# A decoder layer on one core: where the minimum over two key halves and the first experts' pieces stand in the engines' order

## The chip, the core and the metric

The kernel runs on one core of one Trainium2 chip. The metric is the device time of one execution in microseconds (us), the median of three runs. The core has five engines with instruction queues of their own, each worked off in order: TensorE (PE in the profile; its weight loads are shown apart as PEld), VectorE (DVE), ScalarE (ACT), GpSimd (POOL) and SyncE (SP), which here mostly issues DMA transfers. They meet only at semaphores.

## The reference, cut to what matters

One layer with three parts works on x of shape (4, 1024, 256): a gated recurrent scan, a cross attention on a short context, and a transformer block with causal attention and a mixture of experts. The change touches the end of the causal attention and the start of the experts:

```
scores = jnp.einsum('bhqd,bhkd->bhqk', q, k) / hd ** 0.5        # 16 heads of 16
scores = jnp.where(causal, scores, -jnp.inf)
attn = jax.nn.softmax(scores, axis=-1)
o = jnp.einsum('bhqk,bhkd->bhqd', attn, v)...
a = o @ Wo + bo + x
h2 = _ln(a, ln2_g, ln2_b)
logits = h2 @ Wr + br                                            # 8 experts
topv = jax.lax.top_k(logits, TOP_K)[0]                           # 2 of them
w = jax.nn.softmax(jnp.where(logits >= topv[..., -1:], logits, -jnp.inf), axis=-1)
mid = jax.nn.gelu(jnp.einsum('bsd,edf->bsef', h2, e_w1) + e_b1, approximate=False)
moe = jnp.einsum('bse,bsed->bsd', w, jnp.einsum('bsef,efd->bsed', mid, e_w2) + e_b2)
return moe + a
```

## The kernel before, in words

**Stages.** The scan works in eight blocks of 512 tokens (to about 600 us in the profile), the cross attention follows (to about 1050 us), then the causal attention (to about 1877 us), then the experts. All engines but SP run in an order that the program writes out by hand; from the experts' start SP's too.

**Attention units.** A unit is one block of 512 queries (BLK) with a group of four heads (c, four groups); there are 32 units of cross attention and 32 causal ones. Of the eight causal units of a sequence, four belong to its first half of the queries (512 keys) and four to the second (1024 keys). Each unit has two lists of jobs. The *search* (largest) finds for each query the greatest score: matmuls into a score tile of PSUM (ps_max, L825), for the diagonal keys the mask added by DVE (L830), then a reduce on DVE with the sign turned (L832). For the second half of the queries it takes the keys in two parts: results for the first 512 go to m (mpad), those beyond to a tile twice, and the minimum of both (a maximum, as the signs are turned) is L836. Then put() (L834 to L841) transposes m on PE with an identity (shift, L839) and DVE adds the result to the queries (qs, L841). The *weighing* makes the scores again with these shifted queries (ps_exp, L896), takes the exponential on ACT (L898), cuts the diagonal on POOL (L902) and multiplies with the values (ps_o, L866). The search and the score products share three score tiles of PSUM (tag sc).

**Order of jobs.** The main loop runs the weighing of unit u step by step and, beside it, the search of unit u+1, which is ahead by LEAD = 5 jobs (find). put() of a unit is issued as soon as two search jobs of the following unit have been issued:

```
if min(begins[put[0] + 1] + 2, len(search)) <= found[0]:
    units[put[0]][0][1]()
```

The sixteen searches of a unit with 1024 keys are sorted by width and turned by five, so a unit ends and the next one begins with widths of 384, 256 and 128 keys. Around these lists, other jobs (norms, projections, output products, routing) are filled in from the lists ahead, urgent, behind and norms.

**After the last unit.** Twelve jobs with matmuls of the last block remain in urgent and behind: four back (L918), two transposes of on (L758), two output products two (L946, whose sum v DVE adds in L949), two transposes of the normalised rows (L758), choose with the router product (L1280), and places with the ranks (L1308, L1309). Between the eighth and the ninth stand nine jobs without matmuls, the norm of v: four statistics (L1010, L1011), the root (DVE L132, then a power on POOL, L133), its product (L1026), two scalings on ACT (L1032), and an end mark. rows (a DMA on SP, L1260, and copies on POOL) stands ahead of choose; two totals (POOL, L1267) and gates (DVE, L1297 to L1303) stand between choose and places; two totals, place and eight scatters on POOL (sent, L1337) stand behind.

**The first experts' pieces.** Four blocks of 256 rows (firsts_), whose rows are known before the last block is routed, are worked off in pieces between these jobs. A part is two of eight hidden columns (hidden, L1604, with Gelu on ACT, L1607) or four of eight products of the second layer (second, L1614); it counts. A with_ entry counts nothing and follows at once: added (two DVE operations, L1623 and L1624, and a scatter on POOL, L1627), load (five DMA loads on SP, L1551 to L1569), addressed (L1582, L1584) and turned (transposes on PE, L1592, and DVE, L1593). The list holds hidden of blocks 0 and 1 (eight parts), results of 0 and 1 (eight parts, 9 to 16; with added after parts 10, 12, 14 and 16, and load and turn of block 2 after 12, of block 3 after 16), then hidden and results of 2 and 3 (sixteen parts). some(n) issues n counting parts; what is left is issued after the tables of the remaining blocks (L1701 to L1770), and then the main loop over those blocks begins (L1775 on).

## Time and profile before

| | |
|---|---|
| median of three runs | 2412.08 us (2404.89 to 2424.54) |
| profiled execution, its own time | 2414.23 us |
| its span, first to last instruction | 2412.5 us |
| TensorE, mean granted clock | 0.955 |
| busy: TensorE, VectorE, ScalarE, GpSimd | 95%, 55%, 42%, 18% |

All times below are those of the profiled execution, counted from the start of its span. A row of the order of time has start, duration, engine, line, operation, what it writes and reads, and how often it was repeated without a break; in brackets stands how long the engine sat idle before it and what ended that. The granted clock is the share of TensorE's full clock that it was given.

### The profile page before, as it was taken

Reading aid. Unit: us, or ns where it says so; the run is one execution under the profiler, and the core shown is the slowest. Engines: PE = TensorE matmul, PEld = TensorE weight load, DVE = VectorE, ACT = ScalarE, POOL = GpSimd, SP = SyncE. Lnnn points to the kernel's source line nnn. Section 1 sums busy time; section 2 is a strip of 40 time slices with the busy share of each in tenths; the row PEclk is TensorE's granted clock in tenths of the full one; section 3 lists DMA queues with packets and bytes.
Section 4 is the critical chain, followed back from the end, with each engine's and each line's share of the span. In section 5 each row is a group of like instructions: output and inputs, shape, how many; then the busy total and the mean of one; then the engine's idle time right before and its main releaser. Section 6 shows DMA issues by size and latency. Waiting matters only on the chain. (4 is left out here: it accounts for less than half of the span.)

```text
span 2412.5 us, 35625 instructions
## 1 busy us (share of the span) xinstructions
PE 2280.5 (95%) x13356; PEld 1358.8 (56%) x13356; DVE 1315.2 (55%) x2742; ACT 1014.1 (42%) x1541; POOL 440.3 (18%) x642
## 2 busy tenths in 40 slices
PE   6999999998899999999999999999899899999998
PEld 2666666666545555343344334333433678888887
DVE  5767666667545554467667767765866231111111
ACT  3453344443345555354554455354435322222222
POOL 3100000000201011021132224133223222222222
PEclk9999999999889999899999899899989999999999
DMA  8970000000100010000111010001001556766666
GB/s 213 280 194 1 1 1 1 1 1 1 41 19 13 20 27 16 19 23 10 32 32 36 19 36 19 28 27 52 10 27 35 174 156 198 203 193 186 192 203 201
DMA packets 136288, 177.30 MB, mean 73 GB/s; under 512 B 33156, under 2 KB 109292, under 8 KB 136108
## 3 DMA queue, kind: packets, MB, share of 16 engines
q1 hardware_dynamic: 113900, 122.80, 16.5%
q0 software_dynamic: 21696, 51.79, 9.0%
q8 instruction: 109, 1.79, 0.3%
q14 instruction: 71, 0.58, 0.1%
q10 hardware_dynamic: 512, 0.34, 0.1%
HBM read 101.98 MB, written 60.33 MB: 67 GB/s over the span
## 5 line engine op out<-in xcount | busy, mean ns | idle before, releaser
L898 ACT ACTIVATE pt<-ps_exp 128x1024 f32<-128x1024 f32 (+4 forms) x512 | 438.1, 861 | 479.0 <-PE ps_max L825 260.8
L896 PE MATMUL ps_exp<-qs,kT 32*128 32x512 f32 (+4 forms) x2048 | 501.5, 586 | 5.8 <-DVE mpad L832 1.8
L825 PE MATMUL ps_max<-kT,qa 32*128 32x512 f32 (+3 forms) x1536 | 359.1, 559 | 7.5 <-ACT pt L898 3.5
L832 DVE TENSOR_REDUCE mpad<-ps_max 128x2 f32<-128x1024 f32 (+3 forms) x256 | 261.0, 1025 | 96.3 <-PE ps_max L825 91.2
L1607 ACT ACTIVATE mid<-ps,bias 128x256 f32<-128x256 f32 (+1 forms) x296 | 133.0, 459 | 357.9 <-PE ps L1604 335.7
L896 PEld LDWEIGHTS ps_exp<-qs,kT 32*128 32x128 f32 (+1 forms) x2048 | 147.7, 181 | 238.0 <-issue 136.5
L1604 PE MATMUL ps<-hT,w 128*128 128x256 f32 (+1 forms) x1184 | 250.1, 369 | 4.2 <-DVE hT L1593 3.7
L1614 PE MATMUL ps<-w,mid 128*128 128x256 f32 x1104 | 251.4, 381 | 2.1 <-DMA w<-in_L_ffn_e_w_dram 2.1
L866 PE MATMUL ps_o<-pt,vs 128*32 128x512 f32 (+4 forms) x2048 | 246.7, 549 | 2.0 <-POOL pt L902 1.6
L1604 PEld LDWEIGHTS ps<-hT,w 128*128 128x128 f32 x1184 | 214.0, 192 | 33.7 <-DVE hT L1593 4.2
L1614 PEld LDWEIGHTS ps<-w,mid 128*128 128x128 f32 x1104 | 207.4, 191 | 29.2 <-DMA w<-in_L_ffn_e_w_dram 2.7
L902 POOL TENSOR_SCALAR_AFFINE_SELECT pt<-pt 128x256 f32<-128x256 f32 x256 | 104.1, 408 | 526.0 <-ACT pt L898 524.9
L1627 POOL DMA_INDIRECT out_dram<-y,to x69 | 107.1, 1552 | 404.4 <-DVE y L1624 370.7
L814 DVE TENSOR_REDUCE mpad<-ps_max 128x4 f32<-128x616 f32 x128 | 102.2, 800 | 143.7 <-PE ps_exp L896 101.4
L830 DVE TENSOR_TENSOR ps_max<-ps_max,mask_qk 128x256 f32<-128x256 f32 x256 | 109.6, 428 | 89.7 <-PE ps_max L825 81.4
L825 PEld LDWEIGHTS ps_max<-kT,qa 32*128 32x128 f32 x1536 | 124.4, 194 | 58.6 <-ACT pt L898 28.1
L1582 DVE CAST to<-xr 128x2 int32<-128x2 f32 (+1 forms) x37 | 6.1, 166 | 247.1 <-DMA xr<-routed 245.7
L323 PE MATMUL ps_xz<-xnT,w_in 128*128 128x512 f32 x256 | 124.0, 611 | 0.5 <-ACT xnT L315 0.3
L866 PEld LDWEIGHTS ps_o<-pt,vs 128*32 128x32 f32 (+1 forms) x2048 | 42.1, 110 | 132.7 <-issue 103.3
L340 PE MATMUL ps_a<-w,w_a 128*128 128x512 f32 x256 | 115.9, 593 | 0.0
L810 PE MATMUL ps_max<-kT,qa 32*128 32x154 f32 x1024 | 107.0, 331 | 3.4 <-ACT pt L898 1.8
L832 DVE TENSOR_REDUCE twice<-ps_max 128x2 f32<-128x768 f32 (+3 forms) x128 | 105.5, 824 | 4.4
(328 smaller groups left out, 3026.2 us busy)
## 6 DMA issues: line engine op xcount, KB each, us to landing
w<-in_L_ffn_e_w_dram SPq DMA_DIRECT2D x74, 1024.0 KB, 7.2
routed<-zero POOLq DMA_DIRECT2D x16, 2080.0 KB, 53.0
xr<-routed SPq DMA_DIRECT2D x32, 260.0 KB, 6.8
qa<-close SPq DMA_DIRECT2D x248, 32.0 KB, 1.9
last<-in_L_ffn_e_b_dram SPq DMA_DIRECT2D x37, 128.0 KB, 4.0
kT<-close SPq DMA_DIRECT2D x128, 32.0 KB, 2.0
plain<-row SPq DMA_DIRECT2D x8, 512.0 KB, 4.9
out_dram<-xs SPq DMA_DIRECT2D x8, 512.0 KB, 2.9
```

The costliest lines, as they stand in the source:

```text
L323: nc.tensor.matmul(ps, w_in[:, k, c * P : (c + 1) * P], xnT[:, k, :], start=k == 0, stop=k == 1)
L340: nc.tensor.matmul(ps, w_a[:, k, c * P : (c + 1) * P], w[:, k, :], start=k == 0, stop=k == 3)
L825: nc.tensor.matmul(ps[:, i, : s1 - s0], qT[r, j * P : (j + 1) * P], kT[r, c, s0:s1], start=True, stop=True)
L830: nc.vector.tensor_add(x, x, mask_qk.unsqueeze(1).to_broadcast([P, 2, P]))
L832: nc.vector.tensor_reduce(to, ps[:, :, : s1 - s0], AX.X, ALU.max, negate=True)
L866: nc.tensor.matmul(o[0][g * HP : (g + 1) * HP, off:], vs[:n, kt, (4 * c + g) * HV : (4 * c + g) * HV + HP], pts[g // 2][:n, g % 2, off:], ...
L896: nc.tensor.matmul(ps[:n, i, off:], kT[r, c, k0 : k0 + n], shifted[0][r, off:], start=True, stop=True)
L898: nc.scalar.activation(pt[:n, :, off:], ps[:n, :, off:], AF.Exp, scale=HD**-0.5)
L1604: nc.tensor.matmul(ps[:, :mb], self.w1[:, k, f * P : (f + 1) * P], self.hT[:, k, :mb], start=k == 0, stop=k == 1)
L1607: nc.scalar.activation(self.mid[:, f, :mb], ps[:, :mb], AF.Gelu, bias=self.bias[:, f : f + 1])
L1614: nc.tensor.matmul(self.ps, self.mid[:, f, j * P : (j + 1) * P], self.w2[:, f, :], start=f == 0, stop=f == FF // P - 1)
L1627: nc.gpsimd.indirect_dma_start(out=rows, out_offset=bass.IndirectOffsetOnAxis(ap=self.to[:, j_], axis=0), in_=y, in_offset=None, bounds_ch ...
```

## The change

The minimum L836 is taken out of put(). In units with a second key part, the last search job of the unit is wrapped: it runs and then issues the minimum. So on DVE's queue the minimum stands directly behind its unit's last reduce; the transposes and the add of put() stay where they were.

In the loop over the last block's jobs, some() stands ahead of each job with matmuls and no longer behind it, and the list of counts has one entry more: 18 parts are issued in the loop, 17 before.

```
--- before.py
+++ after.py
@@ -831,9 +831,12 @@
                 to = twice[:, j, 2 * pair : 2 * pair + 2] if s0 else m[:, j, 2 * pair : 2 * pair + 2, HD]
                 nc.vector.tensor_reduce(to, ps[:, :, : s1 - s0], AX.X, ALU.max, negate=True)
 
+            def last(job):
+
+                job()
+                nc.vector.tensor_tensor(m[:, :, :, HD], m[:, :, :, HD], twice, ALU.min)
+
             def put():
-                if twice is not None:
-                    nc.vector.tensor_tensor(m[:, :, :, HD], m[:, :, :, HD], twice, ALU.min)
                 tp = mm_tile("shift")
                 for j in range(NJ):
                     nc.tensor.transpose(tp[:, j * P : (j + 1) * P], m[:, j].rearrange("p g i -> p (g i)"), ident)
@@ -852,6 +855,8 @@
                 for i in range(len(parts)):
                     _, j, s0, pair = parts[(i - LEAD) % len(parts)]
                     jobs.append(lambda j=j, s0=s0, pair=pair: many(j, s0, pair))
+            if twice is not None:
+                jobs.append(lambda job=jobs.pop(): last(job))
             return jobs, put
 
         waiting, urgent, ahead, behind = [], [], [], []
@@ -1684,12 +1689,11 @@
                 if not _:
                     n -= 1
 
-        some(1)
-        gaps = [1, 1, 1, 2, 1, 1, 1, 3, 1, 1, 3]
+        gaps = [1, 1, 1, 1, 2, 1, 1, 1, 4, 1, 1, 3]
         for job in urgent + behind:
+            if job.mm:
+                some(gaps.pop(0))
             job.do()
-            if job.mm and gaps:
-                some(gaps.pop(0))
 
         rp = ss.enter_context(tc.tile_pool(name="r_tab", bufs=1))
```

More of the change, by code (lines that the diff above doesn't have):

```diff
@@ L832, in many, with last @@
                 nc.vector.tensor_reduce(to, ps[:, :, : s1 - s0], AX.X, ALU.max, negate=True)
+            def last(job):
+                job()
+                nc.vector.tensor_tensor(m[:, :, :, HD], m[:, :, :, HD], twice, ALU.min)
             def put():
-                if twice is not None:
-                    nc.vector.tensor_tensor(m[:, :, :, HD], m[:, :, :, HD], twice, ALU.min)
                 tp = mm_tile("shift")
@@ L854, in largest @@
                     jobs.append(lambda j=j, s0=s0, pair=pair: many(j, s0, pair))
+            if twice is not None:
+                jobs.append(lambda job=jobs.pop(): last(job))
             return jobs, put
@@ L1685, in some @@
                     n -= 1
-        some(1)
-        gaps = [1, 1, 1, 2, 1, 1, 1, 3, 1, 1, 3]
+        gaps = [1, 1, 1, 1, 2, 1, 1, 1, 4, 1, 1, 3]
         for job in urgent + behind:
+            if job.mm:
+                some(gaps.pop(0))
             job.do()
-            if job.mm and gaps:
-                some(gaps.pop(0))
         rp = ss.enter_context(tc.tile_pool(name="r_tab", bufs=1))
```

## The prediction, made before the changed kernel was run

> **What bounds the kernel now.** I read the page first, then the windows by stage, then the waits and the order of time around the lines that the diff touches. The page says that TensorE (PE) is the bound almost everywhere.

> ```profile
> span 2412.5 us, 35625 instructions
> PE 2280.5 (95%) x13356; PEld 1358.8 (56%) x13356; DVE 1315.2 (55%) x2742; ACT 1014.1 (42%) x1541; POOL 440.3 (18%) x642
> ```

> The min (L836) stands in the causal attention, 1050 to 1862 us. Windows there, one after the min of 1142.4 us, one after that of 1747.2 us, and the expert start (columns: stretch, length, busy time and instructions of PE, PEld, DVE, ACT, POOL, granted clock, DMA share, GB/s):

> ```profile
> 1050.00:1862.00 812.00, 762.65 (x5183) 321.63 (x5183) 568.44 (x1146) 382.04 (x537) 212.32 (x401) 0.94 0.09 27
> 1142.00:1158.00 16.00, 15.38 (x108) 6.36 (x108) 10.89 (x22) 6.68 (x10) 1.51 (x4) 1.00 0.08 17
> 1749.00:1767.00 18.00, 17.49 (x84) 8.25 (x84) 9.92 (x25) 5.03 (x7) 3.14 (x5) 0.53 0.09 30
> 1877.00:1964.00 87.00, 72.12 (x351) 61.07 (x349) 32.70 (x143) 24.44 (x45) 23.40 (x29) 0.92 0.53 155
> ```

> PE is idle for 49 of 812 us, and its clock is sometimes halved: 0.53 over 18 us. The waits (engine, line, releaser; total, times, longest), and one of them in order of time:

> ```profile
> PE shift L839 <- DVE mpad L836: 26.2, 16, 2.3
> PE shift L839 <- ACT close L774: 2.4, 1, 2.4
> ```
> ```profile
> 1786.03 0.42 DVE L830 TENSOR_TENSOR ps_max<-ps_max,mask_qk 128x256 f32<-128x256 f32 x1
> 1786.49 0.69 DVE L832 TENSOR_REDUCE twice<-ps_max 128x2 f32<-128x512 f32 x1
> 1787.10 0.17 DVE L836 TENSOR_TENSOR mpad<-mpad,twice 128x16 f32<-128x16 f32 x1
> 1787.33 0.66 PE L839 MATMUL shift<-ident,mpad 128*128 128x128 f32 x4 [1.57 <-DVE mpad L836]
> 1788.02 0.69 DVE L841 TENSOR_TENSOR qs<-qa,shift 128x512 f32<-128x512 f32 x1 [0.75 <-PE shift L839]
> ```

> The min is ready to run once its unit's last reduce is done (here 1784.8), but it stands behind two search jobs of the next unit. PE has run those two searches and stands at the shift transposes for 1.57 us. Over half of the stage's idle time is these 16 waits. At the expert start PE stands still twice, and the norm starts late:

> ```profile
> 1901.30 0.69 DVE L949 TENSOR_TENSOR v<-v,wo 128x512 f32<-128x512 f32 x1 [2.77 <-PE wo L946]
> 1908.26 0.42 DVE L1010 BATCH_NORM_STATS2 bnst<-v 128x6 f32<-128x256 f32 x1
> 1912.69 1.95 PE L758 MATMUL tp<-ident,row 128*128 128x128 f32 x4 [5.81 <-ACT row L1032]
> 1933.35 0.19 PE L1706 MATMUL n_extra<-extra,ones 128*128 128x1 bf16 x1 [6.10 <-DVE extra L1703]
> 1964.30 0.80 PE L1604 MATMUL ps<-hT,w 128*128 128x256 f32 x1 [2.58 <-DVE hT L1593]
> ```

> **Part 1, the min.** Nothing is added or removed: 16 mins of 0.17 us, each moved ahead of two mask adds (0.42) and reduces (0.69 to 0.96). What it is moved past on DVE is delayed by 0.17 us; PE waits for those reduces only for a free score tile, of which there are three. PE's order is unchanged, and no DMA, ScalarE, SP or POOL instruction moves. (a) The wait. PE reached the transposes 1.2 to 2.0 us before the min, and the last reduce had ended 2.3 to 4.4 us before it, so the whole 26.2 us can go. Next late is DVE: behind the put it runs the shift add (0.69), then mask add and reduce of three short searches (1.1, 0.85, 0.85), 3.5 us, while PE needs about 3.0 for them and already loses 0.2 to 0.6 there. The shift add comes only some 0.9 us earlier, so PE will give part of its 1.6 us back. Bounds 12 and 26; I take 20. The score products that need the shift come over 3 us later, so its add stays covered.

> (b) The clock. The trace's record of the granted clock knows two values, 1 and 0.5. Ten of the sixteen puts are followed, within 6 us of the min, by a stretch at half clock: 10.2, 17.1, 6.8, 6.8, 17.1, 3.4, 6.8, 3.4, 17.1, 10.2 = 98.9 us. Puts without a min are the control: 43 of 48 show no gap at their transposes, four have 0.25 to 0.75 us and no half clock behind them, and one waits 2.4 us for ACT (L774) and has half clock behind it. So in this stage the stretches hang on the waits. One sign is against that: of four router groups (L1280) at full clock three are followed by none, but the one at 1429.2 us stands right ahead of the stretch of 1431.7 us. Their price: 16 router matmuls take 1.95 us at full and 3.58 at half clock, so at most 0.46 of a stretch is lost, 45 us. From first to second put of a batch it is 38.0 us with 10.2 us of half clock and 41.1, 40.9, 39.9 with 17.1: 2.6 us for 6.9, 0.38 each. From second to third, 36.6 with none, 35.9 with 6.8, 36.9 with 3.4: nothing seen. So 71.7 us of long stretches at 0.38 is 27, 27.2 us of short ones at 0.15 (between none and 0.46) is 4: 31 us if all go. Bounds 0 and 45; as the short waits that may be left (0.25 to 0.75) brought none, I take 28.

> [...]

> **Part 2, the pieces.** The last block's jobs hold twelve with matmuls; pieces stood behind each, now in front. Between neighbours that is the same place: ahead of the first eight 1, 2, 3, 4, 6, 7, 8 and 9 pieces are done in both kernels. Ahead of the ninth (row transposes) it is 12 before and 13 after, of the tenth 13 and 14, of the router 14 and 15, of the ranks 17 and 18. What differs in order: pieces 10 to 12 (second-layer products with two added(), the load and the turn of block 2), and one more, stand behind the nine norm jobs and not ahead of them; one piece stands before the router, and three behind the gates. (c) Norm: v is complete at 1901.99, but DVE reaches the statistics at 1908.26, behind two added() (0.42+0.35 each) and the turn (0.16+0.16+0.99), which wait for PE. Now it starts at 1902.0, and the rows end 5.86 us later (as 1908.26 to 1914.12), at 1907.9. PE meanwhile runs four pieces of 1.78 us (24 matmuls took 5.34) and the turn's 0.6, to 1908.8: no wait, 0.9 us to spare. Before, the transposes ended at 1914.64 with three pieces done; now at 1909.4 with four: 5.2+1.8. PE also ran 6.8 us from 1909.6 at half clock (piece 13: 2.88 us against 1.89), another 0.7. Sum 7.7. (d) Ranks no longer wait 0.54 for the turn on DVE, and kept, whole, reciprocal and gate (1927.08 to 1928.25) run ahead of the ranks: 1.1 off the 6.10. Sum 9.3. (e) Given back: the main blocks need the table too. It moves by place, 9.3 less the one piece more that now lies ahead of the ranks, 1.8: 7.5, through eight scatters on POOL (1.27 each) and DVE's table work. The first main rows would be late by up to 1.8, half of it within the 2.58 of PE idle that is there anyway: I take 8.5, bounds 4 (the norm not covered) and 10. On SP the order is the same (load 2, plain rows, load 3, output rows), on POOL the norm's power is ahead of two scatters, and two totals ahead of one; POOL is idle before them. On ACT no Gelu lies in pieces 9 to 16.

> **Sum.** 20 + 28 + 8.5 = 56.5 off the profiled 2414.2 (span 2412.5 and 1.7 around it) is 2357.7; that execution is 2.1 above the median of three, so 2356.

> **The rivals.** A: the half clock stays, brought about by the short, thin matmuls at each unit's end and not by the wait. For it: the router at 1429.2 us, and in the scan a gap of only 0.39 us (PE L381 at 205.05 us, among matmuls with 16 rows of weights) is followed by half clock; against: the 43 puts. Then 20+8.5: 2412-28.5 = 2384. [...] B: the wait is replaced: PE stops one or two matmul groups later, at the score tile that the same two reduces free. For it: DVE is busy 70% of the stage and waits of PE on it are there (0.2 to 0.6). Against: three tiles, of which two are free by then. The puts give 5, the clock nothing: 2412-13.5 = 2398. C, slower: as B, but the wait now lies whole in one of the clock's windows at all 16 puts and not at 10: six more stretches of 17.1 at 0.38 are 39, less the tail's 8.5: 2442. It decides from two more long stretches (13 against 8.5). That the change does not do what it says is left out: the min is issued with its job.

> **How the numbers follow.** Forecast 0.70, with a range of its own of 2335 (26+41+10 off the 2412) to 2378 (20+10+4 off); A 0.15, B 0.10, C 0.05. The range of 8 in 10 reaches to A: 2335 to 2390. One per cent, about what a measurement of this kernel can tell from none (its three runs lie 0.8% apart), is 2388 and 2436. Faster: the forecast and most of A, 0.82; within: the rest of A and B, 0.13; slower: C, 0.05.

> **What would show it.** Right: no wait of the shift transposes on DVE (26.2 before); a granted clock above 0.98 in the attention stage (0.94); transposes of the rows without the 5.81 wait, and 5 us left of the 6.10. Wrong: half-clock stretches behind puts without a wait (A), or a new wait of scores or searches for DVE of 15 to 25 us (B, C).

## The result, and the profile after

The changed kernel takes 2381.89 us (median of four runs, 2381.47 to 2384.16), the kernel before 2412.65 us beside it (2404.89 to 2424.54): a ratio of 0.987, interval 0.983 to 0.991. That is 30.8 us less, inside the range of 2335 to 2390, but 26 us above the forecast of 2356. Run again later, the same kernel took 2381.91 us, and there the ratio was 0.984 (0.980 to 0.989), as the kernel before took 2424.28 on that chip.

The profiled execution after took 2381.52 us. Its page begins:

```profile
span 2379.8 us, 35650 instructions
PE 2266.9 (95%) x13356; PEld 1353.4 (57%) x13356; DVE 1313.7 (55%) x2742; ACT 1013.7 (43%) x1541; POOL 441.1 (19%) x642
```

I compare by stages that begin and end at the same instruction in both kernels. "Causal" runs from the first shift transposes of a causal unit to the first transposes of expert rows. Its windows, before and then after (stretch, length, busy time of PE, PEld, DVE, ACT, POOL, granted clock, DMA share, GB/s):

```profile
1017.10:1877.57 860.47, 809.85 (x5500) 339.44 (x5498) 594.44 (x1206) 413.54 (x581) 228.35 (x429) 0.93 0.10 29
```

```profile
1021.04:1850.56 829.52, 794.46 (x5500) 333.00 (x5499) 592.50 (x1206) 414.48 (x583) 228.55 (x429) 0.96 0.10 30
```

The same 5500 matmuls take 31.0 us less. PE's idle time in them is the length less the busy time: 50.6 us before, 35.1 after, so 15.5 us are waits. The other 15.5 us are busy time, and the change that the trace shows there is the clock: it is at half speed for 114.3 us of this stage before and for 63.0 after (from the trace's record of the granted clock). All stages (PE idle is counted between PE's first and last instruction):

| stage | before: us, PE idle, half clock | after: us, PE idle, half clock | difference |
|---|---|---|---|
| scan | 637.5, 25.3, 45.4 | 640.4, 25.2, 51.3 | +2.9 |
| cross | 379.6, 14.7, 34.9 | 380.6, 14.9, 35.9 | +1.0 |
| causal | 860.5, 50.6, 114.3 | 829.5, 35.1, 63.0 | -31.0 |
| tail, to n_extra | 55.8, 12.6, 10.1 | 52.9, 8.4, 7.0 | -2.9 |
| rest of the experts | 479.1, 5.8, 11.5 | 476.4, 6.4, 5.4 | -2.7 |

These are one profile of each kernel, and the split depends on which execution was taken. The profile of changed_again (the changed kernel once more, below) has 838.6 us for the causal stage, with 37.6 us of PE idle time and 69.9 us of half clock: 21.9 us less than before, 13.0 of them waits. The experiments below widen this. The nine profiles without added matmuls differ in this stage by the place of the min (the late last put of three of them aside). The two with the min late take 860.5 and 869.4 us, the seven with it early 829.5 to 851.0. On the mean the stage is 27.8 us shorter, 17.3 of them PE idle time.

The waits of PE after (engine, line, releaser; total, times, longest); line numbers are up to five higher than before, and the transposes of put() are now L842:

```profile
PE ps_exp L901 <- DVE twice L832: 6.0, 12, 0.9
...
PE n_extra L1710 <- DVE extra L1707: 5.7, 1, 5.7
PE tp L1597 <- DMA xr<-routed: 4.8, 3, 2.1
PE ps_max L825 <- DVE twice L832: 3.5, 5, 1.2
...
PE shift L842 <- DVE mpad L837: 2.1, 1, 2.1
```

Of the sixteen waits of the shift transposes one is left. In its place stand short waits of the score products and searches for the reduces (twice, L832): 9.5 us, against 2.3 before in the two lines below.

```profile
PE ps_exp L896 <- DVE twice L832: 1.5, 3, 0.9
PE ps_max L825 <- DVE twice L832: 0.8, 1, 0.8
```

In order of time, a put of the kernel after (compare the one at 1787.33 before):

```profile
1760.60 0.96 DVE L832 TENSOR_REDUCE twice<-ps_max 128x2 f32<-128x768 f32 x1
...
1761.59 0.18 DVE L837 TENSOR_TENSOR mpad<-mpad,twice 128x16 f32<-128x16 f32 x1
...
1761.69 0.42 DVE L830 TENSOR_TENSOR ps_max<-ps_max,mask_qk 128x256 f32<-128x256 f32 x1
1761.70 0.48 PE L901 MATMUL ps_exp<-qs,kT 32*128 32x256 f32 x2 [0.39 <-DVE twice L832]
...
1762.46 0.66 PE L842 MATMUL shift<-ident,mpad 128*128 128x128 f32 x4
...
1764.08 0.68 DVE L844 TENSOR_TENSOR qs<-qa,shift 128x512 f32<-128x512 f32 x1
...
1765.98 0.38 PE L901 MATMUL ps_exp<-qs,kT 32*128 32x128 f32 x2 [0.79 <-DVE twice L832]
...
1768.64 0.63 PE L871 MATMUL ps_o<-pt,vs 128*32 128x256 f32 x4 [1.60 <-POOL pt L907]
```

The min stands directly behind its unit's last reduce, and the transposes wait for nothing. But 3.5 us later PE waits 0.79 us for a score tile that a later reduce has to free, and at 1768.64 it waits 1.60 us for the cut of an exponential: PE is now ahead of the other engines by what it no longer loses at the transposes, and gives part of that back a little later.

The start of the experts after:

```profile
1875.93 0.69 DVE L954 TENSOR_TENSOR v<-v,wo 128x512 f32<-128x512 f32 x1 [2.77 <-PE wo L951]
1876.54 0.42 DVE L1015 BATCH_NORM_STATS2 bnst<-v 128x6 f32<-128x256 f32 x1
...
1883.08 0.60 PE L758 MATMUL tp<-ident,row 128*128 128x128 f32 x4
...
1885.38 0.38 SPq L1556 DMA_DIRECT2D xr<-routed  x1
...
1893.18 0.63 PE L1597 MATMUL tp<-ident,xr 128*128 128x128 f32 x4 [2.09 <-DMA xr<-routed]
...
1903.41 0.19 PE L1710 MATMUL n_extra<-extra,ones 128*128 128x1 bf16 x1 [5.68 <-DVE extra L1707]
```

The statistics stand right behind v, where 6.3 us lay before, and the transposes of the rows no longer wait 5.81 us. New is the wait of 2.09 us at 1893.18: the turn of block 3 comes earlier on PE, and its rows, whose load is issued at 1885.38, have not landed. The wait ahead of n_extra is 5.68 us, against 6.10.

### The profile page after: what moved, and what is told of

Same layout as the page of the kernel before. It is cut to its first block, busy times and chain, and to the rows that moved or that the text cites. A ratio compares the mean times of both kernels' runs of the same rounds, so it can differ in the third digit from the quotient of the medians.

```text
span 2379.8 us, 35650 instructions
## 1 busy us (share of the span) xinstructions
PE 2266.9 (95%) x13356; PEld 1353.4 (57%) x13356; DVE 1313.7 (55%) x2742; ACT 1013.7 (43%) x1541; POOL 441.1 (19%) x642
## 5 line engine op out<-in xcount | busy, mean ns | idle before, releaser
L901 PE MATMUL ps_exp<-qs,kT 32*128 32x512 f32 (+4 forms) x2048 | 490.6, 572 | 10.2 <-DVE twice L832 6.0
L825 PE MATMUL ps_max<-kT,qa 32*128 32x512 f32 (+3 forms) x1536 | 351.0, 546 | 8.9 <-DVE twice L832 3.5
L832 DVE TENSOR_REDUCE mpad<-ps_max 128x2 f32<-128x1024 f32 (+3 forms) x256 | 261.1, 1025 | 92.6 <-PE ps_max L825 87.3
L871 PE MATMUL ps_o<-pt,vs 128*32 128x512 f32 (+4 forms) x2048 | 240.6, 535 | 3.1 <-POOL pt L907 2.7
L830 DVE TENSOR_TENSOR ps_max<-ps_max,mask_qk 128x256 f32<-128x256 f32 x256 | 109.5, 428 | 83.4 <-PE ps_max L825 76.6
L832 DVE TENSOR_REDUCE twice<-ps_max 128x2 f32<-128x768 f32 (+3 forms) x128 | 105.5, 825 | 4.4
```

Source lines behind the costliest of these rows:

```text
L825: nc.tensor.matmul(ps[:, i, : s1 - s0], qT[r, j * P : (j + 1) * P], kT[r, c, s0:s1], start=True, stop=True)
L830: nc.vector.tensor_add(x, x, mask_qk.unsqueeze(1).to_broadcast([P, 2, P]))
L832: nc.vector.tensor_reduce(to, ps[:, :, : s1 - s0], AX.X, ALU.max, negate=True)
L871: nc.tensor.matmul(o[0][g * HP : (g + 1) * HP, off:], vs[:n, kt, (4 * c + g) * HV : (4 * c + g) * HV + HP], pts[g // 2][:n, g % 2, off:], ...
L901: nc.tensor.matmul(ps[:n, i, off:], kT[r, c, k0 : k0 + n], shifted[0][r, off:], start=True, stop=True)
```

## The experiments

Theory at the start: the gain is the waits (some 16 us net), the clock (some 15 us: short waits of PE take it down, and about half of the stretches had another cause), and the tail (5 to 6 us). Rival: that the clock hangs on how much work the array (128 rows and 128 columns, the most that the weights of any matmul in the profiles fill: 128*128 in their rows) gets, and not on the waiting. Ratios are against the kernel before on the same chip, which took 2424.63, 2420.11 and 2424.28 us (medians) in the three groups of runs.

**Each part alone.** min_alone has the first half of the diff, pieces_alone the second.

> The kernel before with the min moved to its unit's last search job, the pieces as before. Theory (the wait and the clock are separate terms, the tail a third): the shift transposes' wait on DVE falls from 26.2 to the last unit's 2.1 us, idle time of the attention stage by about 15, half clock there from 102 to about 55 us, and the time by 20 to 28 us, to 2385 to 2393. Rival (the gain of 31 us sits mostly in the pieces): under 12 us.

> The kernel before with the pieces moved, the min as before. Theory: the 5.81 us wait of the row transposes goes, the wait of n_extra falls to 5, and the time falls by 8 to 9 us, to about 2404; attention as before, its half clock near 100 us. Rival (the min's gain comes from a luckier phase of the clock, which any shift of the program can bring): half clock in the attention stage falls by 20 us or more without the min.

min_alone: 2397.95 us, 0.987 (0.984 to 0.990), 26.7 us less. pieces_alone: 2419.25 us, 0.997 (0.994 to 1.000), 5.4 us less. Together they make 32 us. The time of min_alone lies in the expected 20 to 28 us; pieces_alone gives less than the expected 8 to 9. The waits are parted as the kernels are, as expected. First min_alone, then pieces_alone:

```profile
PE n_extra L1711 <- DVE extra L1708: 6.1, 1, 6.1
PE tp L758 <- ACT row L1037: 5.8, 1, 5.8
...
PE shift L842 <- DVE mpad L837: 2.1, 1, 2.1
```

```profile
PE shift L839 <- DVE mpad L836: 24.6, 15, 2.3
...
PE n_extra L1705 <- DVE extra L1702: 4.8, 1, 4.8
```

So the min part carries most of the gain. The clock did not come out as expected in min_alone: its profile has 97.1 us of half clock in the causal stage, where I had expected about 55, and 8.7 us less idle time than before, where I had expected 15. That execution is the longest of the four (2409.44 us). Up to the last unit the order of work is that of the kernel after, whose profile has 63.0. It has two single waits, 5.2 us of ps_exp for ACT and 3.3 us of ps_max for DVE, that the profiles of before and after lack. In pieces_alone the stage keeps its half clock (116.1 us), so the rival, that any shift of the program takes it away, falls.

**The wait filled instead of taken away.** dense_fill is the kernel before, with matmuls that nobody reads ahead of the sixteen transposes; the transposes write over them. thin_fill has the same with 32 rows of weights in place of 128.

```
                 tp = mm_tile("shift")
+                if twice is not None:
+                    for _ in range(2):
+                        nc.tensor.matmul(tp, ident, qT, start=True, stop=True)
```

```
+                        nc.tensor.matmul(tp, ident[:HP, :], qT[:HP, :], start=True, stop=True)
```

> The kernel before, the min where it was, with two matmuls of 128x512 through all 128 rows (0.6 us each) ahead of the transposes in each of the 16 puts with a min; their result is overwritten by the transposes. They lie inside the wait (1.4 to 2.3 us), so the chain is not shorter, but PE idles only 0.3 to 1 us there. Theory (half clock hangs on PE's idle time at the puts, and has a price of its own): half clock in the attention stage falls from 102 to 60 us or less and the time falls by 10 to 15 us, to 2398 to 2403. Rival 1 (half clock comes from the short, thin matmuls around, not from the wait): half clock stays near 100 us, time 2412. Rival 2 (half clock has next to no price, as DVE sets the pace there): half clock falls, time stays 2412.

> As dense_fill, but the two matmuls use 32 of the 128 weight rows: PE is as busy by the clock on the wall, the array a quarter as much. Theory (idle time by the clock on the wall is what counts): as dense_fill, 2398 to 2403 us. Rival (the gate counts work in the array): half clock stays near 80 to 100 us and the time near 2410.

dense_fill: 2398.71 us, 0.990 (0.986 to 0.993), 25.9 us less. thin_fill: 2403.39 us, 0.990 (0.987 to 0.993), 21.2 us less. The min is as late as before in both; PE only does useless work in place of standing still, and the kernel is faster by nearly as much as with the min moved. Causal stage of dense_fill, then of thin_fill:

```profile
1011.82:1855.17 843.35, 809.23 (x5564) 338.80 (x5562) 593.95 (x1206) 413.25 (x581) 228.42 (x429) 0.98 0.10 30
```

```profile
1011.45:1865.30 853.85, 817.04 (x5564) 341.09 (x5562) 594.37 (x1206) 413.18 (x581) 228.44 (x429) 0.96 0.10 31
```

PE idles 34.1 and 36.8 us here, about as long as in the kernel after. The half clock is 31.9 us with dense fills and 63.5 with thin ones, of 114.3 before. So the waits did bring the clock down here, as the filled kernel shows without moving anything. But at about equal idle time the fill with 128 rows leaves half as much of it as the one with 32. So in these two profiles the waiting alone does not set the clock; the half clock differs with the rows that the fills use, too. I had expected 10 to 15 us of the dense fill and the same of the thin one, and it is more in both.

Part of the fills' gain lies where nothing was edited: the cross attention took 374.0 and 373.1 us, against 379.6 in the profile of before. The causal stage itself gained 17.1 us with dense fills and 6.6 with thin ones.

**Dense fills on the changed kernel.** after_dense adds the lines of dense_fill to the kernel after.

> The changed kernel with the two dense matmuls of dense_fill ahead of the transposes of each of the 16 puts with a min. Here 15 of them have no wait to fill, so they cost 15 x 1.2 = 18 us of PE. Theory (what is left of the half clock hangs on little work in the array at the ends of the units): half clock in the causal attention falls from 63 to about 32 us, as in dense_fill, worth 10 us at 0.3 each; net 6 to 10 us slower than the changed kernel, about 2390. Rival (it hangs on the short waits for DVE that are left, which the fill does not touch): half clock stays near 63 us, 18 us slower, about 2400.

2392.77 us, 0.987 (0.982 to 0.993): 10.9 us above the 2381.89 of the changed kernel. Its causal stage has 33.0 us of idle time and 49.0 us of half clock, between what the two theories gave (32 and 63). By the medians the 32 extra matmuls, with one wait left to fill, cost more than the clock they save; its four runs spread from 2379.97 to 2401.07 us, and the intervals of the ratios overlap.

**The router.** Half clock that is left after begins at 1063.5, 1111.3, 1319.5, 1418.5, 1527.7, 1596.0, 1633.6, 1729.1 and 1852.0 us (3.4 to 10.2 us each; the last one belongs to the tail, and one that begins at 1015.7 us, in the cross attention, reaches into the stage). Three of these (1319.5, 1418.5, 1527.7) begin no more than 1.3 us from the end of a router product, 16 matmuls with 8 columns (L1285; one runs from 1316.51 to 1318.46). They come at the same places of the program in min_alone, last_put_late, rows3_early and all_four. So: dense matmuls ahead of the router, on the kernel after (router_dense), and together with dense_fill on the kernel before (both_fills).

```
+                for k in range(2):
+                    nc.tensor.matmul(ps, ident, hb()[:, k, :], start=True, stop=True)
```

> The changed kernel with two dense matmuls of 128x512 (1.2 us together) ahead of each of the eight router products, whose 16 matmuls have only 8 columns each; the router overwrites what it reads. In the changed kernel half clock begins 1.1 and 1.3 us behind the routers of 1316.5 and 1524.5 us and inside the one of 1416.7 us, 6.8 us each. Theory (matmuls of few columns are little work for the gate, whatever the waits): these three stretches go, half clock in the causal attention falls from 63 to about 43 us; 5 us gained at 0.27 each, 8.4 us paid for the fill of seven routers there, so 3 us slower. Rival (the stretches come from the short waits at the unit's end, some us before): they begin at the same places.

> The kernel before with both fills, two dense matmuls ahead of the transposes of each put with a min and two ahead of each router. Theory: half clock in the causal attention falls below the 32 us of dense_fill, to 20 us or less; the time is that of dense_fill within 5 us. Rival (half clock there has further causes of the same weight): it stays at 30 us or more.

router_dense: 2399.22 us, 0.991 (0.988 to 0.994), 17.3 us above the changed kernel beside it (2381.91). both_fills: 2411.18 us, 0.995 (0.993 to 0.997), 12.5 us above dense_fill, where I had expected the same within 5. The causal stage of both_fills, where I had expected at most 20 us of half clock:

```profile
1011.07:1876.77 865.70, 830.08 (x5593) 344.99 (x5591) 594.03 (x1206) 413.79 (x581) 228.95 (x429) 0.97 0.10 31
```

It is 53.1 us. In router_dense the three stretches behind the routers are gone, but others stand at 1390.7 and 1602.3 us, where changed_again has none (the second is where the profile of after has the one of 1596.0), and the sum is 58.0 instead of 69.9 us. The stage takes 847.2 us, 8.6 more than in changed_again: seven fills of 1.98 us in it are 13.9, which 11.9 us less of half clock do not pay for. I had expected 3 us more in all. In both_fills a stretch of 20.5 us begins at 1419.1, 1.1 us behind a router product that had dense matmuls ahead of it. So a fill ahead of a router product does not reliably keep the clock up, and the theory that it would falls. That these products bring the clock down is not refuted by it: in both_fills 0.59 of the 1.98 us of the fill lie in the 3.41 us ahead of the stretch (the last part on the clock below).

In router_dense the cross attention, ahead of every edit, took 388.4 us with 57.4 us of half clock. Windows of the cross attention in both_fills, in before and in router_dense (2650 matmuls, one record more or less, and no edit ahead of them in any):

```profile
637.82:1011.07 373.25, 359.08 (x2650) 181.89 (x2649) 190.92 (x358) 195.10 (x251) 39.03 (x54) 0.97 0.08 20
```

```profile
637.47:1017.10 379.63, 364.90 (x2650) 184.44 (x2649) 191.09 (x358) 195.19 (x251) 38.97 (x54) 0.95 0.08 20
```

```profile
636.97:1025.38 388.41, 374.47 (x2649) 189.03 (x2648) 191.28 (x358) 195.43 (x251) 38.96 (x54) 0.93 0.08 19
```

With 21.7, 34.9 and 57.4 us of half clock. This is a price that no edit blurs: a line through all fourteen profiles gives 0.42 us of cross attention for each us of half clock. In the causal stage, PE's idle time taken off, the nine profiles without fills give 0.26.

**The one wait that was left.** It is the last unit's (2.1 us): no unit follows, so its put comes directly behind its last search job, with or without the change. last_put_late issues that put two steps of weighing later.

```
-                if min(begins[put[0] + 1] + 2, len(search)) <= found[0]:
+                if put[0] + 1 < len(units) and begins[put[0] + 1] + 2 <= found[0]:
...
+            if found[0] == len(search) and put[0] + 1 == len(units):
+                over.append(u)
+                if len(over) == 3:
+                    units[put[0]][0][1]()
+                    put[0] += 1
```

> The changed kernel with the put of the very last unit two steps later. This unit has no following search jobs, so before and after the change its put comes right behind its last search job and PE waits 2.08 us for min and reduce. Theory: that wait goes (no wait of the shift transposes on the min is left) and the time falls by about 2 us, which a comparison can hardly tell; the trace must show it. Rival: the wait moves to the score products of the last unit, since the shifted queries are late, and the gain is nothing.

2381.81 us, 0.983 (0.979 to 0.987). The wait for the min is gone (0.6 us for another operation of DVE, L1320, stands in its place), and the time is that of the changed kernel: the difference is less than these runs tell apart.

**The late rows of block 3.** rows3_early issues the load of its rows right behind the loads of block 2, ahead of the plain rows on SP.

```
+                with_(firsts_[2].load)
+                with_(firsts_[3].early_rows)
...
+                with_(lambda: firsts_[3].load(rows=False))
```

> The changed kernel with the row load of the fourth expert block moved up on SP, to behind the loads of the third. In the changed kernel it stands behind the store of the plain rows, is issued at 1885.38 us and lands at about 1893, and PE waits 2.09 us for it. Theory (this new wait gave back a part of the pieces' gain): the wait goes, ranks and n_extra come 2 us earlier, the time falls by 1 to 2 us. Rival: PE only waits longer at n_extra (5.7 to 7.7 us), nothing gained.

2381.49 us, 0.984 (0.980 to 0.989). The load is issued ahead of the plain rows, and the wait of 2.09 us is gone; the wait ahead of n_extra is 6.65 us, where it was 5.68:

```profile
1883.27 0.37 SPq L1553 DMA_DIRECT2D xr<-routed  x1
1883.75 0.60 SPq L1265 DMA_DIRECT2D plain<-row  x1
...
1890.14 0.50 PEld L1606 LDWEIGHTS tp<-ident,xr 128*128 128x128 f32 x4
1890.28 0.60 PE L1606 MATMUL tp<-ident,xr 128*128 128x128 f32 x4
...
1901.46 0.19 PE L1723 MATMUL n_extra<-extra,ones 128*128 128x1 bf16 x1 [6.65 <-DVE extra L1720]
```

Half of what one wait gives goes into the next. From the first expert transposes to n_extra the time is 49.9 us, against 52.9 after and 50.9 in changed_again. The 1 to 2 us that I had expected cannot be told apart in the kernel's time.

**All of it.** all_four takes last_put_late, the early rows, three pieces between the ranks and n_extra, and the counting constants of the tables (on POOL) ahead of the loop. The expectation does not name the early rows; the kernel has them.

```
+        count(f"at{MB // 2}", NTOK // MB, MB)
+        count("at0", NTOK // MB, MB)
+        count("num", NB - NE + NX, 1)
...
+        some(3)
```

> The changed kernel with the last put two steps later, three pieces more issued between ranks and n_extra, and the three iotas of the last tables issued on POOL ahead of the last block's jobs and not behind its eight scatters. Theory: PE no longer idles 5.7 us at n_extra, DVE no longer waits 8.3 us for the iotas, so the tables are ready early and the main blocks start as soon as PE is through the pieces: 2 us from the last put and 5 to 7 us at the tables, to about 2374. Rival (the main blocks wait for the scatters' landing and the row load, not for the tables): PE's idle time moves to the first main block, gain 2 us, 2380.

> The kernel of all_four once more, beside the changed one on the same chip. It holds the early row load of rows3_early too, beside the late last put, the three pieces ahead of n_extra and the early iotas. Theory: 5 us faster than the changed kernel, as the two medians differ that were taken apart. Rival: the difference was one of chips, under 2 us.

> The changed kernel once more, beside the others on their chip: ratio to before 0.985 (between the 0.987 first measured and 0.9872 x 0.9971 of its two parts alone); half clock in the causal attention 55 to 70 us.

all_four: 2376.7 us, 0.981 (0.977 to 0.986); again, beside the changed kernel: 2377.34 us, 0.981 (0.976 to 0.986), against 2381.91 us, 0.984 (0.980 to 0.989). It beats the kernel before clearly. all_four lies between its theory (2374) and its rival (2380); the 4.6 us of all_four_again to the changed kernel agree with the expected 5, but the intervals overlap. What it does at the end of the tail is plain (all_four_again):

```profile
1896.49 0.63 PE L1613 MATMUL tp<-ident,xr 128*128 128x128 f32 x4 [1.26 <-DMA xr<-routed]
1907.35 0.18 PE L1740 MATMUL n_extra<-extra,ones 128*128 128x1 bf16 x1 [1.03 <-DVE extra L1736]
```

PE's idle time from the first expert transposes to n_extra is 2.9 us in both runs, 8.4 in the kernel after; the pieces stand where it waited.

## Why the prediction was right or wrong

The direction, the place and the kinds of gain were right; the size was about half (30.8 us of 56.5) beside the first runs of the kernel before, and three quarters (42.4) beside those of changed_again. The time of 2382 lies outside the forecast's own range (2335 to 2378). It lies inside 2335 to 2390 because that range was stretched to reach rival A, and that is luck as far as the mechanism goes. Of the signs of being right, the granted clock of the stage is missing: 0.96, not above 0.98. Step by step, by the two profiled executions, with changed_again beside them:

- **(a) The wait of the transposes: 20 forecast, 15.5 came (13.0 by changed_again, 17.3 by the means of nine profiles).** Two sizes were off. Not "the whole 26.2 us can go" but 24.1: the last unit has no successor whose searches could stand between, and its put waits 2.1 us in both kernels. And the new waits for reduces are 7.2 us (9.5 against 2.3), with 1.1 us more at ps_o, where I had allowed 6 in all. 24.1 less 8.3 is 15.8; other waits in the stage changed too, so that this meets the 15.5 so closely is in part chance. A part of rival B is thus true: PE stops again a few matmul groups later, but for a third of the wait and not for most of it.
- **(b) The clock: 28 forecast, some 15 came (8.9 by changed_again).** This is the step that failed. The price was near: I had 31 us for 98.9 us, 0.31 each; the traces give 15.5 us for 51.3, 0.30, 8.9 for 44.3 by changed_again, 0.20, and 0.26 over nine profiles. What failed is "in this stage the stretches hang on the waits", that all of them behind the puts would go. Of 102 us of half clock between 1050 and 1862 us 54 are left. Seven of the nine stretches there, 47.8 us, begin 4.0 to 8.5 us behind a put with a min whose transposes waited for nothing: the sign of being wrong that I had named. The control that I leaned on, 43 puts without a gap, was weaker than I took it to be. Of these puts 32 lie in the cross attention, among matmuls of other shapes, one (750.6 us) is followed by half clock 5.3 us later, and four begin inside a half-clock stretch. The sign against it that I had named, a router right ahead of a stretch, was worth more than I gave it: three of the seven begin within 1.3 us of the end of a router product, with no idle time of PE in the 3.41 us ahead of them.
- **(c) The norm: right.** v at 1875.93, statistics at 1876.54, transposes without a wait. The wait that I said would not come there did not come.
- **(d) and (e) The tail: 8.5 forecast, 5.6 came (2.9 to n_extra and 2.7 behind it).** The bounds were 4 and 10; by changed_again it is 8.2, so the size is not settled to better than that. What the forecast lacked is 2.09 us of waiting for the rows of block 3 ahead of n_extra, whose own wait was 5.68 where I had 5. I had written "on SP the order is the same", which is so, and had not asked whether PE's earlier turn would find the rows there. pieces_alone gives 5.4 us by medians, which agrees with the 5.6 but has an interval of 1 to 13 us.
- **What I had not in the sum:** the scan and the cross attention took 3.9 us longer in the profile after, with 6.9 us more of half clock and no edit in them; in changed_again they took 4.2 us less than before. The sum of the stages is 31.0 + 5.6 - 3.9 = 32.7, and the spans differ by 32.6.

The rivals: the time, 2382, lies beside that of A (2384), but A's sum is not what happened: in A the clock gives nothing and the wait 20; here the clock gave about 0.4 to 0.5 of the causal gain. A's cause, thin matmuls and not the wait, agrees with a part: the three stretches at the routers. C did not occur: behind the puts PE's waits are shorter, and the half clock fell. For the windows of the clock that C speaks of the traces have the intervals of 3.413 us in the next part: in the profile of before six of the sixteen waits lie whole in one of them, not ten, and behind each of the six half clock begins within 3.5 us of the interval's end. Filling waits of 1.4 to 2.3 us took the half clock of the causal stage from 114.3 to 31.9 us in dense_fill (53.1 in both_fills), so in this kernel waits of that length cost clock.

| stage of all fourteen profiles | intervals at half clock: all, behind one below 1550 | intervals at full clock: all, behind one below 1550 |
|---|---|---|
| causal (the bound was chosen here) | 271, 267 | 3186, 38 |
| cross | 131, 130 | 1406, 70 |

In the profiles of before and after alone it is 50 of 51 at half clock and 5 of 442 at full clock in the causal stages, 18 of 18 and 10 of 202 in the cross attention. Idle time alone parts them badly: of the 119 falls of the clock in the causal stages, 37 follow an interval in which PE idled for 0.05 us at most. The three stretches behind routers in the profile after are of this kind: the intervals ahead hold the router product and count 1370, 1437 and 1447 with no idle time. Its four other stretches between 1100 and 1800 us follow intervals with 0.75 to 1.4 us of short waits and counts of 1208 to 1342. As it is made up, the count falls with a wait, with weights of 32 rows and with products of 8 columns alike, and a fill raises it only in the interval in which it lies: in both_fills the fill ran from 1414.33 to 1416.31 us, and the interval behind which the 20.5 us begin started at 1415.72. How the chip itself sets the clock is not shown.

**What stays open:** the count is fitted to the traces of this one program, with matmul times that the trace models; no run was made to test it, and some intervals do not fit. As the place of the intervals is not known before a run, it does not say ahead of time which stretch an execution will have. Sixteen executions of the kernel before on one chip took 2406.91 to 2429.02 us, with mean granted clocks of 0.963 and 0.954 in these two.

## What to carry to other kernels

An operation that ends a unit belongs directly behind what it needs, not at the place that uses it: on a queue worked off in order, whatever stands between is a wait for somebody else (here 26.2 us of PE, in sixteen waits). When such waits are taken away, price the clock as a term of its own, in the stage where it changes, and count only those stretches as won for which a control among the same shapes of matmuls shows that the wait is what brings them on and that nothing else nearby does (here half clock stood behind router products, too). Take more than one profile: the cross attention, with no edit in it, took 373.1 to 388.4 us, in step with its half clock. For each step that moves forward, ask of its DMA as well whether it will be there (here PE waited 2.09 us for one), and look at the last unit of a loop by itself.

## What was not expected of the hardware

- Useless dense matmuls in place of a wait made the kernel 25.9 us faster, with the wait's cause untouched; with a quarter of the rows they left 63.5 us of half clock in the causal stage and not 31.9.
- The price of half clock differs by stage: 0.42 us for each us in the cross attention, 0.26 in the causal stage. At a router product it had been 0.46. That other engines set the pace more often in the causal stage would explain it, and is not shown: DVE is busy for 71% of it after (592.5 of 829.5 us) and for about half of the cross attention (190.9 of 373.3 us in both_fills).
- A stage that no edit touches took 373.1 to 388.4 us over the profiles, in step with its half clock (21.6 to 57.4 us). A difference of 15 us in one profile can thus be the clock of another stage: parts have to be compared by stage, and a fill's or an edit's gain against that.
